# Attention and triangle layers on one core: the first scores of the second head pair moved to a later place in the first period

## The chip, the cores and the metric

The kernel runs on one core of a Trainium2 chip. The metric is the device time of one execution in microseconds; three executions of the kernel before took 3711.04, 3712.01 and 3713.63 us, so the median is 3712.01 us. The engines are named as the profile names them: PE is TensorE (PEld its weight loads), DVE is VectorE, ACT is ScalarE, POOL is GpSimd, SP is SyncE, which here issues most of the transfers.

## The reference

Two layers run one after the other on x of shape (4, 64, 64, 256), in float32. Layer 0 is self-attention over the 4096 tokens of each of the four images. Layer 1 treats each 64 x 64 image as a grid of pairs and lets edges (i, l) and (l, j) meet:

```python
# layer 0
f = xt @ Wf + bf ; g = xt @ Wg + bg ; v = xt @ Wh + bh
beta = softmax(einsum('bqd,bkd->bqk', g, f), axis=-1)
x = x + (einsum('bqk,bkd->bqd', beta, v) @ Wo + bo).reshape(b, h, w, c)
# layer 1: 8 heads of 32
q, k, v1, v2 = (x @ W).reshape(B, N, N, H, d_k) for W in (Wq, Wk, Wv1, Wv2)
scores = einsum('bilhd,bljhd->biljh', q, k) / sqrt(d_k)
att = softmax(scores, axis=2)
out = einsum('biljh,bilhd,bljhd->bijhd', att, v1, v2)
h = layer_norm(x + out.reshape(B, N, N, E) @ Wo)
h = layer_norm(relu(h @ W1 + b1) @ W2 + b2 + h)
```

## The kernel before

**Stages.** The four images go through one after the other. For each, `layer0` computes the attention (8 blocks of 512 tokens) and writes y, q, k, v1 and v2 of layer 1 to DRAM. Then a *triangle stage* computes layer 1's scores, weights and triple product for that image. In the first triangle stage (`first_layer1`) the projections of the later images' layer 0 are computed alongside. In the other three (`next_layer1`) the layer norms and the perceptron of the previous image run alongside. The last image's norms and perceptron follow on their own at the end (`alone`).

**The triangle stage.** The 8 heads form 4 pairs, the 64 rows i form 8 groups: 32 steps. Each step makes eight products (`product`, word R, L955): DVE or POOL multiplies a 128 x 64 slice of weights by a 128 x 2048 block of v2 into a tile. DVE's tiles are R (three buffers), POOL's are Rp (two). `accumulate` (word A, L965) contracts each product over l on PE into one of two PSUM tiles "acc" per step, one for products 0 to 3, the other for 4 to 7. `take` (word T, L975) copies an acc out by ACT. POOL makes products 5 to 7 of step 0 in every stage.

**Weights.** `sums` (word S) adds up a step's exponentials on DVE, `weights` (W) scales them on ACT into "es", `turn_weights` (t) transposes them on PE, `copy_weights` (c) copies POOL's share out as attP, and `stationary` (V) fills the stationary operand from v1 and fetches a later step's v1.

**Scores.** `scores` (word sp, L853) computes a quarter of a pair's scores with 64 small matmuls into a PSUM tile "sp". `take_scores` (words e, L863) writes its two halves through Exp to the tile S on ACT. The pair's q and k are fetched by `fetch_qk` (L820, L823). Pair 0's scores are made at the end of `layer0`. The fetch of pair 1's q and k is issued there too, near the end, after the last scores of pair 0 have been issued, since both pairs use the same two buffers. Word sp of period 1 is the first quarter of pair 1.

**The order.** Nothing reorders the work: each engine runs what the program gives it in that order. The order is written out by hand as lists of words, `ORDER` for stages two to four (a period is two steps) and `ORDER0` for the first (four steps). A word's number after the slash is how many periods late it runs: in period p, "A05/1" accumulates product 5 of step 0 of period p - 1. Period 0 of a stage has almost nothing to do, as most words are one or two late. Period 1 is the first with products. In it the words that act are, in order, for stages two to four:

```
R05 S1 sp e0 e1 A05 R04 A04 z0 W1 R03 V1 S0 z1 t1 so R06 R00 c1 sa A03 R07 R02 A06
A02 A00 rr pp W0 R01 A07 A01 fo fa T01 R12 t0 T00 R17 h1 R13 h0 ht R16 hU A13 ...
```

Words of the alongside work here: z0, z1 are the perceptron's output matmuls (L1177), so (ACT) and sa (DVE, L1040) the norms' statistics, rr, pp the inverse roots on ACT and their polishing on POOL, fo, fa the norms' affine maps on ACT, h0, h1 the heads (L1024), ht the turning of the normed tile (L1124), hU and hT its shift and scale. In the first stage the words from the scores on are `sp0 e00 e01 P00 C00 t1 R00 P01 C01 R03 A00 R02 g0 a0 b0 R05 R07 A05 A03 ...`: P turns a fetched block of the next image, xin, on PE (L345), C copies it out (L350), g, a and b are its projections (PE L234, ACT L243, DVE L248).

**Buffers that bear on the order.** PSUM tiles of tag "a" have two slots, taken in turn by sp and acc. The three R buffers of DVE are, at the end of `layer0`, the "stage" tiles from which the last block's q, k, v1 and v2 are stored to DRAM; a product can take one only when its stores have ended.

Of the kernel before, what the change touches and what calls it, by code (L numbers as in the profile page):

```python
# [40 lines left out]


ORDER = """
    r0/1 A10/2 A11/2 m1/1 R14/2 R05/1 S1/1 R15/2 T10/2 sp/1 A14/2 A16/2 r1/1 e0/1 e1/1 A15/2 A05/1 T11/2
    R04/1 A04/1 z0/1 W1/1 R03/1 V1/1 fi/2 S0 z1/1 t1/1 so/1 R06/1 R00/1 c1/1 sa A03/1 R07/1 R02/1 A06/1
    A02/1 A00/1 rr/1 pp/1 W0 R01/1 A07/1 A01/1 fo/1 fa T01/1 R12/1 t0 T00/1 R17/1 h1/-1 R13/1 h0/-1 ht
    R16/1 hU A13/1 hT A12/1 A17/1 R11/1 c0 R10/1 m0 V0
""".split()


# [5 lines left out]
    A21/2 g1/2 S3/1 W1/1 A27/2 A23/2 A26/2 a1/2 V3/2 A24/2 P31/2 C21/2 R32/2 b1/2 m1/2 T20/2 c3/2 P30/2 C31/2  # L56
    t0/1 v2/2 n1/2 R25/2 A25/2 R33/2 sp0/1 T21/2 A32/2 C30/2 R34/2 R36/2 R30/2 A33/2 e00/1 u2/2 e01/1 o1/2 R31/2
    g2/2 P00/1 c0/1 R37/2 A34/2 A36/2 A30/2 A31/2 A37/2 V0/1 R35/2 C00/1 T30/2 t1/1 R00/1 p1/2 P01/1 a2/2 b2/2
    C01/1 A35/2 R03/1 T31/2 A00/1 R02/1 g0/1 a0/1 b0/1 R05/1 R07/1 A05/1 A03/1 v3/2 R06/1 u3/2 m0/1 S2/1 W2/1
    c1/1 v0/1 V1/1 R01/1 A02/1 n0/1 R04/1 A07/1 A01/1 A04/1 R12/1 P11/1 u0/1 P10/1 A06/1 T00/1 sp1/1 C11/1 T01/1  # L60
    R13/1 R15/1 R14/1 A13/1 e10/1 e11/1 t2/1 C10/1 R10/1 A12/1 R17/1 V2/1 A15/1 A14/1 A10/1 R16/1 R11/1 S0 R22/1
    W3/1 g3/2 c2/1 W0 A17/1 R27/1 A11/1 v1/1 R20/1 a3/2 b3/2 u1/1 o0/1 p0/1 S1 R21/1 T10/1 P20/1 t3/1 P21/1
    A16/1 T11/1 C20/1 A20/1 R23/1 A22/1 R24/1 R26/1
""".split()


# [1 line left out]
def attention_then_triangle_kernel(  # L68
# [1264 lines left out]
    def words_of(order):  # L1333
        for w in order:
            w, late = (w.split("/") + ["0"])[:2]
            yield w, int(late)

    def first_layer1(L, ahead, F):
        turned = {}
        ahead.load(0)  # L1340

        def fetched(step):
            if 24 <= step < 31:
                ahead.fetch(F, 1, step)

        own = Late(L)
        step_word, scores, take_scores = step_words(
            L, fetched, lambda step: None, lambda step: ahead.spread(F, 1, step), own
        )

        def front_word(w, s, cc):
            if not 0 <= s < ahead.n:
                return
            if w == "P":
                ahead.turned(s, cc)
                turned[s] = turned.get(s, 0) + 1
                if turned[s] == 2:
                    ahead.load(s + 1)
            elif w == "C":
                ahead.taken(s, cc)  # L1360
            elif w == "v":
                ahead.values(s)
            elif w == "u":
                ahead.valued(s)
            elif w == "g":
                ahead.factors(s)
            elif w == "a":
                ahead.factored(s)
            elif w == "b":
                ahead.parted(s)  # L1370

        for period in range(NSTEP // 4 + 3):
            for word, late in words_of(ORDER0):
                i, last = period - late, int(word[-1])
                if word[0:2] == "sp":
                    if i >= 0:
                        scores(2 * i + last)
                elif word[0] == "e":
                    if i >= 0:
                        take_scores(2 * i + int(word[1]), last)  # L1380
                elif word[0] in "RATSWVtc":
                    step_word(word[0], 4 * i + int(word[1]), last)
                elif word[0] in "mnop":
                    if 0 <= i < 4:
                        own.word(word[0], 2 * i + last)
                elif 0 <= i < 4 and int(word[1]) < 2:
                    front_word(word[0], 2 * i + int(word[1]), last)
                elif 4 <= i < 8:
                    front_word(word[0], 4 * i - 8 + int(word[1]), last)
        ahead.fetch(F, 1, NSTEP)  # L1390


    def next_layer1(b, L, rest, ahead, F):
        own = b == NB - 1
        t0 = NP * (b - 1)


        n2, n1, n0 = NP, NP + own, NP + 2 * own
        stored, held = set(), []
        mv, rs, rn, mps = {}, {}, {}, {}  # L1400

        def fetched(step):
            if F is not None and 24 <= step < 31:
                ahead.fetch(F, b + 1, step)


        def load(q, far=False):
            if q < NP or 24 + (q - NP) // 2 in stored:
                rest.load(t0 + q, far)
            else:  # L1410
                held.append((q, far))

        def was_stored(step):
            stored.add(step)
            if own and step == 26:
                held.extend((NP + q, True) for q in (2, 3, 4))
            todo, held[:] = list(held), []
            for q, far in todo:
                load(q, far)

        def moments(q):
            if q not in mv:
                mv[q] = small.tile([P, 4, 2], F32, tag="mv", name="mv")
            rest.mv = mv[q]

        def of_piece(word, q):
            tt = t0 + q
            first, second = 1 <= q < n1, 0 <= q < n2
            if word in ("h0", "h1"):
                if 2 <= q < n0:  # L1430
                    n = int(word[1])
                    rest.heads(tt, n, new=q not in mps)
                    mps.setdefault(q, {})["h", n] = True
                    if len(mps[q]) == 2 and q + 1 < n0:
                        load(q + 1)
            elif word == "sa" and first:
                moments(q - 1)
                rest.stats(rest.hps[t0 + q], 0)
            elif word == "so" and second:
                moments(q)  # L1440
                z = rest.z[t0 + q] = work.tile([P, 2, C], F32, tag="s4", name="z")
                rest.sums_of(rest.zp[t0 + q], z, rest.mv, 2)
            elif word == "rr" and second:
                moments(q)
                rest.roots(0 if q + 1 < n1 else 2, 4)
                rs[q] = rest.rs
            elif word == "pp" and second:
                moments(q)
                rest.rs = rs.pop(q)
                rest.polish(0 if q + 1 < n1 else 2, 4, nc.gpsimd, back=back_t)  # L1450
                rn[q] = rest.rn
            elif word == "fa" and first:
                rest.rn = rn[q - 1]
                rest.affine_a(tt)
            elif word == "fo" and second:
                rest.rn = rn[q]
                rest.affine_o(tt)
            elif word == "ht" and first:
                rest.turn(tt)
            elif word == "hT" and first:  # L1460
                rest.normed(tt)
            elif word == "hU" and first:
                rest.carried(tt)
            elif word in ("m0", "m1") and first:
                n = int(word[1])
                mps[q][n] = [rest.hidden(tt, fc) for fc in (2 * n, 2 * n + 1)]
            elif word in ("r0", "r1") and first:
                n = int(word[1])
                for fc, mp in zip((2 * n, 2 * n + 1), mps[q][n]):
                    rest.rectify(tt, fc, mp)  # L1470
            elif word in ("z0", "z1") and second:
                n = int(word[1])
                rest.outputs(tt, n, new=tt not in rest.zp)
                mps.setdefault(q, {})["z", n] = True
            elif word == "fi" and second:
                rest.finish(tt)

        def spread(step):
            if F is not None:
                ahead.spread(F, b + 1, step)  # L1480

        step_word, scores, take_scores = step_words(L, fetched, was_stored, spread)
        mps[1] = {}
        for period in range(NP + 4):
            for word, late in words_of(ORDER):
                i = period - late
                if word[0] in "RATSWVtc":
                    step_word(word[0], 2 * i + int(word[1]), int(word[-1]))
                elif word == "sp":
                    scores(i)  # L1490
                elif word in ("e0", "e1"):
                    take_scores(i, int(word[1]))
                else:
                    of_piece(word, i)
        assert not held
        if F is not None:
            ahead.fetch(F, b + 1, NSTEP)
# [68 lines left out]
```

## Time and profile before

| what | value |
|---|---|
| median of three executions | 3712.01 us |
| the profiled execution, its own time | 3709.58 us |
| its span, first to last instruction | 3707.8 us |
| mean granted clock of PE | 0.990 |
| DVE, POOL busy, shares of the span | 71%, 48% |
| DMA mean rate over the span | 87 GB/s |

A triangle stage is not evenly loaded. In the middle of the second one, from 1343.4 to 1640 us, PE is busy for all 296.6 us, DVE for 287.1 and POOL for 284.4, and the granted clock is 1.00. Before it, from 1280 to 1343.4, PE is busy for 54.5 of 63.4 us. The chain of waits is followed back from the last instruction, and each of its pieces says what the next one waited for. In a timeline, a line is a run of like instructions with its start, its length, its engine and line, and in brackets how long the engine was idle ahead of it and what ended that.

### The profile page before, as it was taken

What the parts mean: (1) busy time and instruction counts of PE and PEld (TensorE: products, weight loads), DVE (VectorE), ACT (ScalarE), POOL (GpSimd) and SP (SyncE); (2) the same over time, 40 slices, a digit from 0 to 9 for tenths busy, and PEclk for the clock granted to TensorE, in tenths of its full rate; (3) what the DMA queues carried; (4) which work ended last, traced back from release to release, by engine and by line L of the source; (5) the groups of instructions that cost most, each with busy time, mean ns of one, the idle gap of its engine ahead of it and who ended that gap; (6) DMA issues with size and microseconds to landing.
All of it is one profiled execution on the core that took longest, in us unless ns stands there. A gap on an engine that the chain in (4) does not pass through costs nothing.

```text
span 3707.8 us, 58485 instructions
## 1 busy us (share of the span) xinstructions
PE 3579.3 (97%) x22602; PEld 1932.9 (52%) x22602; DVE 2641.4 (71%) x2078; ACT 1917.9 (52%) x4257; POOL 1761.7 (48%) x918
## 2 busy tenths in 40 slices
PE   9999899989999999998999999999899999999998
PEld 6555444444555555554455555554355555555477
DVE  4555499996555479999555449999755455999976
ACT  3333456554333367675433347676533435677654
POOL 5000199895000069999100019999700005999920
PEclk9999999999999999999999999999999999999999
DMA  9111566566111344425311153333511125432221
GB/s 149 47 46 46 138 163 165 147 160 158 51 51 49 102 107 94 97 51 97 74 49 51 48 142 89 75 90 65 117 42 50 51 70 138 97 89 51 68 65 56
DMA packets 461232, 324.01 MB, mean 87 GB/s; under 512 B 299984, under 2 KB 418512, under 8 KB 451600
## 3 DMA queue, kind: packets, MB, share of 16 engines
q1 hardware_dynamic: 411904, 293.21, 29.8%
q0 software_dynamic: 36160, 19.94, 4.7%
q10 hardware_dynamic: 12880, 7.01, 0.7%
q8 instruction: 181, 2.97, 0.3%
q14 instruction: 107, 0.88, 0.1%
HBM read 176.37 MB, written 143.65 MB: 86 GB/s over the span
## 4 chain that ended last, share of the span: by engine, by line
PE 80%; POOL 9%; DMA 4%; issue 3%; DVE 3%; ACT 1%; SPq 0%; ACTq 0%; POOLq 0%; DVEq 0%
PE o L552 24%; PE acc L965 17%; PE proj L609 8%; POOL Rp L955 7%; PE s L531 6%; PE mp L1157 5%; PE zp L1177 5%; PE sp L853 3%; PE hp L1024 2%; PE v1p L641 2%; PE y L594 2%; DVE R L955 1%; PE att L907 1%; DMA k<-k 1%; PE den L569 1%
## 5 line engine op out<-in xcount | busy, mean ns | idle before, releaser
L955 POOL TENSOR_TENSOR Rp<-attP,v 128x2048 f32<-128x2048 f32 x328 | 1491.3, 4574 | 432.0 <-ACT attP L915 354.0
L955 DVE TENSOR_TENSOR R<-att,v 128x2048 f32<-128x2048 f32 x696 | 1548.8, 2274 | 111.0 <-PE acc L965 67.6
L552 PE MATMUL o<-e,v 128*128 128x512 f32 x2048 | 920.5, 592 | 0.0
L559 DVE TENSOR_TENSOR esum<-esum,e 128x2048 f32<-128x2048 f32 x224 | 512.9, 2290 | 485.8 <-ACT e L541 482.8
L965 PE MATMUL acc<-R,wsel 128*32 128x512 f32 x5568 | 701.6, 601 | 16.1 <-DVE R L955 7.9
L541 ACT ACTIVATE e<-s 128x1024 f32<-128x1024 f32 x512 | 496.9, 1026 | 323.5 <-PE s L531 163.4
L552 PEld LDWEIGHTS o<-e,v 128*128 128x128 f32 x2048 | 388.5, 190 | 391.5 <-issue 369.8
L1085 POOL TENSOR_SCALAR nt<-mv 128x4 f32<-128x4 f32 (+1 forms) x51 | 9.8, 193 | 1216.5 <-DVE mv L1041 1204.1
L531 PE MATMUL s<-gT,fT 128*128 128x512 f32 x1024 | 374.1, 486 | 8.2 <-ACT e L541 4.9
L965 PE MATMUL acc<-Rp,wsel 128*32 128x512 f32 x2624 | 348.1, 603 | 20.7 <-POOL Rp L955 20.1
L975 ACT COPY ao<-acc 128x1024 f32<-128x1024 f32 x256 | 254.6, 1021 | 177.9 <-PE acc L965 167.1
L965 PEld LDWEIGHTS acc<-R,wsel 128*32 128x32 f32 x5568 | 155.2, 110 | 357.3 <-issue 280.9
L531 PEld LDWEIGHTS s<-gT,fT 128*128 128x128 f32 x1024 | 191.9, 190 | 143.7 <-issue 107.5
L890 ACT ACTIVATE es<-S,rd 128x64 f32<-128x64 f32 x1024 | 257.8, 336 | 15.9 <-DVE rd L882 14.4
L571 DVE RECIPROCAL rec<-den 128x512 f32<-128x512 f32 x32 | 107.4, 3357 | 214.4 <-PE den L569 214.4
L1157 PE MATMUL mp<-hT,w 128*128 128x256 f32 x1024 | 249.5, 389 | 0.7 <-ACT hT L1129 0.7
L1177 PE MATMUL zp<-w,hid 128*128 128x256 f32 x1024 | 245.3, 385 | 0.8 <-ACT hid L1166 0.8
L1157 PEld LDWEIGHTS mp<-hT,w 128*128 128x128 f32 x1024 | 186.9, 190 | 101.1 <-ACT attP L915 36.0
L1177 PEld LDWEIGHTS zp<-w,hid 128*128 128x128 f32 x1024 | 186.1, 191 | 63.9 <-issue 30.2
L621 ACT COPY st<-proj 128x512 f32<-128x512 f32 x98 | 57.5, 587 | 304.9 <-PE proj L609 169.8
L965 PEld LDWEIGHTS acc<-Rp,wsel 128*32 128x32 f32 x2624 | 81.0, 110 | 201.5 <-issue 128.6
L863 ACT ACTIVATE S<-sp 128x512 f32<-128x512 f32 x128 | 130.0, 1119 | 98.2 <-PE sp L853 98.2
(176 smaller groups left out, 3597.9 us busy)
## 6 DMA issues: line engine op xcount, KB each, us to landing
v<-v2d SPq DMA_DIRECT2D x44, 512.0 KB
v1c<-v1d SPq DMA_DIRECT2D x128, 128.0 KB
aT<-ao SPq DMA_DIRECT2D x1024, 16.0 KB
A<-aT SPq DMA_DIRECT2D x256, 64.0 KB
out_dram<-z SPq DMA_DIRECT2D x63, 256.0 KB
y<-yT SPq DMA_DIRECT2D x56, 256.0 KB
q<-st SPq DMA_DIRECT2D x56, 256.0 KB
k<-k SPq DMA_DIRECT2D x28, 512.0 KB
```

The lines of the kernel that those rows point to most:

```text
L531: nc.tensor.matmul(s_ps[r // 2][:, r % 2, :], fT[tt][:, ts(r * 4 + n, P)], gT[qb // 4][:, ts(qb % 4, QB)], start=True, stop=not safe,)
L541: nc.scalar.activation(e[g][:, 2 * j : 2 * j + 2, :], s_ps[j], AF.Exp)
L552: nc.tensor.matmul(o_ps[qb], F.v[tt][:, r * 4 + n, :], es[:, r, :], start=(k == 0 and r == 0), stop=(k == 7 and r == 3),)
L559: nc.vector.tensor_tensor(esum[qb], esum[qb], es, ALU.add)
L609: nc.tensor.matmul(ps, w[:, cc, rows], y(qb, cc), start=(cc == 0), stop=(cc == 1))
L863: nc.scalar.activation(self.S[pair][:, :, l0 : l0 + 8].rearrange("p i l -> p l i"), sp[:, lh], AF.Copy if self.safe else AF.Exp,)
L890: nc.scalar.mul(e[:, i, :], rows[:, i, :], rec[:, i : i + 1])
L955: eng.tensor_tensor(R, src.unsqueeze(1).to_broadcast([P, D, N]), v2[h], ALU.mult)
L965: nc.tensor.matmul(acc[32 * c : 32 * c + 32, n % 2, :], w[:, n, c, 16 * h : 16 * h + 32], R[:, ts(c, 8), :].rearrange("p d j -> p (d j)"), ...
L975: nc.scalar.copy(self.ao[step][:, ts(np, 2)].rearrange("p k d j -> p k (d j)"), self.acc[step][np])
L1157: nc.tensor.matmul(self.mp[:, fc % 2, :], w1_sb[:, cc, ts(fc, P)], self.hT[tt][:, cc, :], start=(cc == 0), stop=(cc == 1),)
L1177: nc.tensor.matmul(zp[:, n, :], self.hid[tt][:, fc, ts(n, P)], w2_sb[:, fc, :], start=(fc == 0), stop=(fc == 3 and tt not in self.hT2),)
```

## The change

The word sp of the first period is split off. The first quarter of pair 1's scores now has words of its own, sf with f0 and f1 for its two evictions (sf0, f0, f1 in the first stage). They act only where the quarter is the first, and sp, e0 and e1 act on all quarters but that. In `ORDER`, sf stands after T00, f0 after R13, f1 after ht. In `ORDER0`, sf0 stands ahead of A00, f0 after g0, f1 after R05. All other words keep their order.

```diff
 ORDER:
-    r0/1 ... S1/1 R15/2 T10/2 sp/1 A14/2 A16/2 r1/1 e0/1 e1/1 A15/2 A05/1 ...
-    ... fa T01/1 R12/1 t0 T00/1 R17/1 h1/-1 R13/1 h0/-1 ht R16/1 hU A13/1 ...
+    r0/1 ... S1/1 R15/2 T10/2 sp/1 A14/2 A16/2 r1/1 e0/1 e1/1 A15/2 A05/1 ...
+    ... fa T01/1 R12/1 t0 T00/1 sf/1 R17/1 h1/-1 R13/1 f0/1 h0/-1 ht f1/1 R16/1 hU A13/1 ...
 ORDER0:
-    ... C01/1 A35/2 R03/1 T31/2 A00/1 R02/1 g0/1 a0/1 b0/1 R05/1 R07/1 A05/1 ...
+    ... C01/1 A35/2 R03/1 T31/2 sf0/1 A00/1 R02/1 g0/1 f0/1 a0/1 b0/1 R05/1 f1/1 R07/1 A05/1 ...
 first_layer1:
                 if word[0:2] == "sp":
-                    if i >= 0:
+                    if 2 * i + last > 0:
                         scores(2 * i + last)
                 elif word[0] == "e":
-                    if i >= 0:
+                    if 2 * i + int(word[1]) > 0:
                         take_scores(2 * i + int(word[1]), last)
+                elif word[0:2] == "sf":
+                    if i == 0:
+                        scores(0)
+                elif word[0] == "f":
+                    if i == 0:
+                        take_scores(0, last)
 next_layer1:
-                elif word == "sp":
-                    scores(i)
-                elif word in ("e0", "e1"):
-                    take_scores(i, int(word[1]))
+                elif word in ("sp", "sf"):
+                    if (i == 0) == (word == "sf"):
+                        scores(i)
+                elif word in ("e0", "e1", "f0", "f1"):
+                    if (i == 0) == (word[0] == "f"):
+                        take_scores(i, int(word[1]))
```

More of the change, by code (lines that the diff above doesn't have):

```diff
@@ L43 @@
 ORDER = """
[L44 to L47, printed above, removed]
+    r0/1 A10/2 A11/2 m1/1 R14/2 R05/1 S1/1 R15/2 T10/2 sp/1 A14/2 A16/2 r1/1 e0/1 e1/1 A15/2 A05/1 T11/2 R04/1
+    A04/1 z0/1 W1/1 R03/1 V1/1 fi/2 S0 z1/1 t1/1 so/1 R06/1 R00/1 c1/1 sa A03/1 R07/1 R02/1 A06/1 A02/1 A00/1
+    rr/1 pp/1 W0 R01/1 A07/1 A01/1 fo/1 fa T01/1 R12/1 t0 T00/1 sf/1 R17/1 h1/-1 R13/1 f0/1 h0/-1 ht f1/1 R16/1
+    hU A13/1 hT A12/1 A17/1 R11/1 c0 R10/1 m0 V0
 """.split()
@@ L58 @@
     g2/2 P00/1 c0/1 R37/2 A34/2 A36/2 A30/2 A31/2 A37/2 V0/1 R35/2 C00/1 T30/2 t1/1 R00/1 p1/2 P01/1 a2/2 b2/2
[L59 to L63, printed above, removed]
+    C01/1 A35/2 R03/1 T31/2 sf0/1 A00/1 R02/1 g0/1 f0/1 a0/1 b0/1 R05/1 f1/1 R07/1 A05/1 A03/1 v3/2 R06/1 u3/2
+    m0/1 S2/1 W2/1 c1/1 v0/1 V1/1 R01/1 A02/1 n0/1 R04/1 A07/1 A01/1 A04/1 R12/1 P11/1 u0/1 P10/1 A06/1 T00/1
+    sp1/1 C11/1 T01/1 R13/1 R15/1 R14/1 A13/1 e10/1 e11/1 t2/1 C10/1 R10/1 A12/1 R17/1 V2/1 A15/1 A14/1 A10/1
+    R16/1 R11/1 S0 R22/1 W3/1 g3/2 c2/1 W0 A17/1 R27/1 A11/1 v1/1 R20/1 a3/2 b3/2 u1/1 o0/1 p0/1 S1 R21/1 T10/1
+    P20/1 t3/1 P21/1 A16/1 T11/1 C20/1 A20/1 R23/1 A22/1 R24/1 R26/1
 """.split()
```

## The prediction

> **What bounds the kernel now.** I read the page's busy shares first, then the chain that ended last, then TensorE's waits, and then the timelines of TensorE and VectorE around the first period of each triangle stage.
>
> ```profile
> PE 3579.3 (97%) x22602; PEld 1932.9 (52%) x22602; DVE 2641.4 (71%) x2078; ACT 1917.9 (52%) x4257; POOL 1761.7 (48%) x918
> ...
> PE 80%; POOL 9%; DMA 4%; issue 3%; DVE 3%; ACT 1%; SPq 0%; ACTq 0%; POOLq 0%; DVEq 0%
> ```
>
> TensorE (PE) is busy for 97% of the span and carries 80% of the chain. An idle microsecond of PE is therefore a microsecond of the kernel, unless something else is late just after it. PE's longest wait in total:
>
> ```profile
> PE sp L853 <- DMA k<-k: 29.2, 8, 4.6
> ```
>
> These are eight waits of the scores matmuls for q and k of the second head pair, two in each of the four triangle stages: 5.5 us in the first stage, 7.7, 8.0 and 7.9 in the others. The scores are the "sp" that the change moves. PE's timeline, second stage:
>
> ```profile
> 1317.49 0.38 PE L1029 MATMUL hp<-ident,yc 128*128 128x128 f32 x2
> 1321.10 0.38 PE L853 MATMUL sp<-q,k 32*64 32x64 f32 x2 [3.22 <-DMA k<-k]
> 1325.99 2.02 PE L853 MATMUL sp<-q,k 32*64 32x64 f32 x62 [4.51 <-DMA k<-k]
> 1327.94 1.63 PE L965 MATMUL acc<-Rp,wsel 128*32 128x512 f32 x8
> ...
> 1336.62 1.90 PE L965 MATMUL acc<-R,wsel 128*32 128x512 f32 x16
> ...
> 1343.36 1.07 PE L965 MATMUL acc<-R,wsel 128*32 128x512 f32 x8
> ```
>
> The reader should see PE stop at 1317.87 and go on at 1325.99. The question is what PE could do in that time. VectorE (DVE), same stretch:
>
> ```profile
> 1314.56 4.49 DVE L955 TENSOR_TENSOR R<-att,v 128x2048 f32<-128x2048 f32 x2 [3.92 <-DMA yc<-y]
> ...
> 1326.95 2.29 DVE L955 TENSOR_TENSOR R<-att,v 128x2048 f32<-128x2048 f32 x1 [7.07 <-DMA v2d<-stage]
> ...
> 1330.15 0.18 DVE L1041 BATCH_NORM_AGGREGATE mv<-st 128x2 f32<-128x6 f32 x1
> 1330.51 2.29 DVE L955 TENSOR_TENSOR R<-att,v 128x2048 f32<-128x2048 f32 x1 [0.18 <-PE acc L965]
> ```
>
> DVE stands still for 7.07 us in the same gap, for another transfer. Its third product (R00) needs the third R buffer. That one still holds "stage", whose last store (v2d<-stage, issued by ScalarE at 1316.36) ends at 1326.9. In the third and fourth stage this wait is 7.16 and 7.01 us and ends at 2215.33 and 3105.42, each 0.7 us after the scores got their data. The first stage has another wall, in the chain of waits:
>
> ```profile
> 440.02 12.60 DMA xin<-in_x_dram
> 452.62 0.14 issue
> 452.76 1.09 PE tp L345 x4
> ```
>
> The word after the scores there (P00, the turning of xin) waits for xin, which lands at 452.62. The scores end at 452.6, so they fill a wait that is there anyway.
>
> [...] nothing of PE's later work fills the gap. [...] from 1318 to 1322.2 the engines are busy by 1.01 of their time at 215 GB/s, with the q and k loads, the A loads and the v2d store under way. Moving a matmul does not make that store land earlier. [...]
>
> ```profile
> 1322.30:1329.00 6.70, 3.01 (x70) 2.25 (x74) 2.05 (x1) 0.94 (x2) 1.31 (x1) 0.50 0.64 132
> 1329.10:1331.00 1.90, 1.90 (x15) 0.71 (x8) 1.65 (x6) 1.89 (x6) 1.24 (x1) 0.99 0.75 206
> ```
>
> These are two stretches of the busy table: a stretch, its length, the busy time of PE, PE's weight loads, DVE, ScalarE and GpSimd, then the granted clock, the DMA share and GB/s. The clock is 0.50 until 1329. After the stall it stays at half for 4.8 us in the first stage, and for 3.1, 5.4 and 6.1 us in the others. At half clock the scores' 64 small matmuls cost what they always do (1.9 to 2.0 us), but a group of eight accumulations takes 1.7 us, not 0.87.
>
> **The change part by part.** No instruction is added or removed. 64 matmuls (1.91 us) and two Exp evictions (1.99 us) move, once per stage. The scores issue no DMA (only every fourth quarter does), so SyncE's and GpSimd's queues keep their order. The S that they feed is first read by sums of step 8, in the second period of stage one and the fourth of the others, behind three later quarters, so being late costs nothing by itself.
>
> *Stages two to four* (numbers of the second). Without the scores PE is free at 1317.87. The first accumulation, A05, needs the first of GpSimd's two products, begun at 1314.61 and 9.00 us long together: 1319.1. Then A05 and A04 (0.87 + 0.97), both output words z (3.99), t1 (0.53), A03 and A06 (0.89 + 0.85) bring PE to 1327.3. ScalarE is idle there for 11.72 us and does W1 earlier, so t1 finds its weights. Next is A02, which needs R02. DVE has to do R00 first, not before 1326.95 (2.2), the norm statistics (to 1330.3), and R02 (2.25): 1332.6. So PE waits anew, some 5.4 us, now for DVE. From 1332.7: A02, A00, A07, A01 took 3.55, t0 0.5, the moved scores 1.91, the heads 2.16, ht 0.53. A13 starts at 1341.35 instead of 1343.36: a gain of 2.0, not 7.7. Third stage: the statistics end at 2218.7, R02 at 2220.95, A13 at 2229.7 instead of 2233.11, gain 3.4. There R02 had waited 1.54 us for a PE at half clock, which goes. Fourth: 3119.8 instead of 3123.53, gain 3.7. Together 9.1 us.
>
> The clock takes part of it back. The new idle stretch of 5.4 us is as good for a fall as the old one, and what follows it now is accumulation, not scores. With the clock at half for 3.1 to 6.1 us, half of that time is lost: 1.5 to 3.1 us a stage, I take 2.4, 7.2 in all. Bounds: 0, if the clock doesn't fall, and 10. Net for these stages: -1.9 us.
>
> The scores' PSUM slot ("a", two slots) is now the one that A05 to A07 filled, so they wait for T01 on ScalarE, behind rr, the GpSimd polish and fo, fa. By the same durations T01 ends at about 1336.2, 0.5 us before it is needed: nothing, with up to 2 us a stage if that cover is gone.
>
> *First stage.* P00 stays at 452.76, and P01 ends at 455.43 as before. Then come the scores (1.92), so A00 starts at 457.35, not 455.43: 1.9 us lost, as they no longer fill the wait. More follows: A05 takes the PSUM slot that the scores hold until f1. On ScalarE f1 stands behind a0, which needs g0's matmuls, behind A00. A00 ends at 458.2 (459.05 at half clock), g0 0.9 later, a0 0.65, f1 1.0: A05 at 460.8 to 461.6 instead of 457.19. The chain runs through A05 (457.37, acc x16), so this goes to the end: +3.6 to +4.4, I take 4.0. Floor 1.9, ceiling 5.
>
> **Sum:** 4.0 - 9.1 + 7.2 = +2.1 us. The profiled execution took 3709.58 us (span 3707.8, 1.8 outside it), 2.4 below the median of 3712.01. On the median the forecast is 3714.1.
>
> **Rivals.** (a) The waits for k go and nothing takes their place: 29.2 us, and some 4 us of half clock, 3712 - 33 = 3679. For it speaks PE's 97%. Against it stand DVE's 7.07 us in the same gap and xin. Chance 0.05. (b) The v2d store lands some 3 us or more earlier, or DVE's lag is met by less PE idling, and the clock doesn't fall: stages two to four give 4 to 7 us each, 3695 to 3704, take 3700. [...] Against: no transfer ahead of that store is moved. Chance 0.08. (c) Slower: the moved scores sit in stages two to four behind T01, PE waiting for ScalarE's chain before them. It decides when T01 ends later than 1336.7. With 2 us a stage on top of the forecast: 3714.1 + 6 = 3720. For it: only 0.5 us of cover, and fo waits for the polish. Against: the same order of words had no such wait before, and half clock delays the matmuls as much. Chance 0.17. (d) My forecast, gain and loss nearly cancel: 0.70.
>
> **How the numbers follow.** This kernel can tell 0.2% (7.4 us) from no change. (a) and (b) are faster: 0.13. (d) stays within: 0.70. (c) is slower: 0.17. With stage one at 1.9 and no fall of the clock (d) ends at 3704.8; with both at their ceilings at 3718. The range that leaves a tenth on each side: 3705.5 to 3720.
>
> **What would show it.** Right: PE's waits for k at about 5 us of 29 (the first scores of a stage, if at all); a new wait of A02 for DVE, about 5 us in each of the stages two to four, with clock 0.50 after it; R00 still ending its wait for v2d<-stage near 9 us after the last heads; in the first stage tp waiting 8 us for xin, and A05 1.5 us for ScalarE's S. Wrong: DVE's R00 starting at once, no fall of the clock, or A05 in the first stage at its old distance from P00.

## The result, and the profile after

| | before | changed |
|---|---|---|
| median of 20 executions each, same chips | 3713.59 us | 3715.12 us |
| lowest, highest | 3710.88, 3717.55 us | 3710.02, 3718.76 us |
| span of the profiled execution | 3707.8 us | 3714.7 us |

The ratio of the times is 1.0004, with a 95% interval of 0.9998 to 1.001: between 0.7 us faster and 3.7 us slower, so no change that this measurement can tell. The two profiled executions lie 6.9 us apart, more than the medians do. The changed one (3716.47) was 1.4 us above its median, the other (3709.58) 4.0 us below.

The page of the changed kernel, its busy shares and its chain:

```profile
PE 3583.0 (96%) x22602; PEld 1932.3 (52%) x22602; DVE 2640.8 (71%) x2078; ACT 1918.6 (52%) x4257; POOL 1761.1 (47%) x918
...
PE 80%; POOL 8%; DMA 4%; DVE 3%; issue 3%; ACT 1%; SPq 1%; ACTq 0%; POOLq 0%; DVEq 0%
```

PE's waits (total in us, times, longest), first one line of the kernel before, then those of the changed one:

```profile
PE acc L965 <- DVE R L955: 7.9, 15, 1.4
```

```profile
PE acc L965 <- POOL Rp L955: 24.6, 22, 2.7
PE acc L965 <- DVE R L955: 23.0, 19, 5.3
PE tp L345 <- DMA xin<-in_x_dram: 10.0, 2, 8.0
```

Of the 29.2 us that PE waited for k nothing is left. In their place stand 15.1 us more for DVE's R (23.0 against 7.9), with one wait of about 5 us in each of the stages two to four, and one wait of 8.0 us for xin in the first stage. PE's timeline in the second stage's first period:

```profile
1328.13 0.38 PE L1029 MATMUL hp<-ident,yc 128*128 128x128 f32 x2
1329.84 1.07 PE L965 MATMUL acc<-Rp,wsel 128*32 128x512 f32 x8 [1.33 <-POOL Rp L955]
...
1337.10 1.04 PE L965 MATMUL acc<-Rp,wsel 128*32 128x512 f32 x8
1343.45 3.50 PE L965 MATMUL acc<-R,wsel 128*32 128x512 f32 x16 [5.30 <-DVE R L955]
```

After the last heads (hp, up to 1328.51) PE now waits 1.33 us for POOL's product and then does 8.3 us of work without a pause. Then it stands for 5.30 us, at A02. The 16 accumulations that follow (A02, A00) take 3.50 us; in the kernel before they took 1.90. DVE in the same stretch:

```profile
1325.19 4.49 DVE L955 TENSOR_TENSOR R<-att,v 128x2048 f32<-128x2048 f32 x2 [3.92 <-DMA yc<-y]
...
1337.84 2.29 DVE L955 TENSOR_TENSOR R<-att,v 128x2048 f32<-128x2048 f32 x1 [7.32 <-ACT z L1059]
...
1341.13 11.06 DVE L955 TENSOR_TENSOR R<-att,v 128x2048 f32<-128x2048 f32 x5
```

R00 starts 7.3 us late, as before, 12.65 us after the first two products began (12.39 in the kernel before). The name of the releaser has changed: ScalarE's z here and in the third stage, v2d<-stage in the fourth stage of this same profile. Such a name is the event that came last by the profile, so it need not be the cause; the runs e4 and e5 below decide which of the two it is. The first stage, PE, with A05 in the kernel before ahead of the changed kernel's lines:

```profile
457.19 1.04 PE L965 MATMUL acc<-Rp,wsel 128*32 128x512 f32 x8
```

```profile
453.49 1.09 PE L345 MATMUL tp<-ident,xin 128*128 128x128 f32 x4 [8.01 <-DMA xin<-in_x_dram]
...
456.21 2.03 PE L853 MATMUL sp<-q,k 32*64 32x64 f32 x64
458.18 1.55 PE L965 MATMUL acc<-R,wsel 128*32 128x512 f32 x8
459.55 0.61 PE L234 MATMUL gf<-xT,wg 128*32 128x128 f32 x16
459.99 0.61 PE L234 MATMUL gf<-xT,wf 128*32 128x128 f32 x16
462.32 1.06 PE L965 MATMUL acc<-Rp,wsel 128*32 128x512 f32 x8 [1.72 <-issue]
```

P00 waits 8 us for xin. From P00 to A05 it is now 8.83 us (462.32 less 453.49); it was 4.43 (457.19 less 452.76). Some 0.5 us of that is the clock: A00 ran at half in this profile (1.55 us, granted clock 0.50 up to 459.1), and at full in e2, e7 and e11 (1.06 to 1.07), where P00 to A05 took 8.35. The timeline puts A05's wait down to nothing it knows ("issue"); ScalarE's shows what stands there:

```profile
458.33 1.04 ACT L863 ACTIVATE S<-sp 128x512 f32<-128x512 f32 x1 [1.42 <-PE sp L853]
460.67 0.37 ACT L243 ACTIVATE gf<-gf,bias_g 128x128 fp32r<-128x128 f32 x1 [1.31 <-PE gf L234]
460.94 0.36 ACT L243 ACTIVATE gf<-gf,bias_f 128x128 fp32r<-128x128 f32 x1
461.19 1.03 ACT L863 ACTIVATE S<-sp 128x512 f32<-128x512 f32 x1
```

Between f0 at 458.33 and f1 at 461.19 ScalarE waits 1.31 us for PE's gf. f1 ends at 462.2, and A05 starts at 462.32: it takes the PSUM slot that f1 has just emptied.

**Where the time went, stage by stage.** If the start of each matmul in one trace is set against that of the same matmul in the other, the distance between the two runs can be followed through the kernel (us, changed less before):

```
just behind the first layer 0       +0.9
after the first stage's period 1    +5.2
at the start of the second stage   +10.6
behind the second stage's period 1 +10.5
behind the third's                  +8.4
behind the fourth's                 +7.3
```

The first stage costs 4.3 us in its first period and 5.4 later, the second stage gives 0.1, the third 2.2, the fourth 1.1 with the end of the third and the layer 0 ahead of it. So in these two profiles the small sum is made of two parts of opposite sign.

Of the loss later in the first stage, the larger part falls at one place, some 425 to 435 us behind layer 0's end: 3.6 us of a wait, and the half clock behind it (0.50 from 847.7 to 851.4; in the kernel before the same matmuls ran at 1.00). The kernel before, then the changed one:

```profile
838.78 2.05 PE L357 MATMUL vp<-wh,xT 128*128 128x128 f32 x16 [1.92 <-ACT va L364]
```

```profile
847.67 3.78 PE L357 MATMUL vp<-wh,xT 128*128 128x128 f32 x16 [5.49 <-ACT va L364]
```

```profile
846.52 0.37 ACT L243 ACTIVATE gf<-gf,bias_g 128x128 fp32r<-128x128 f32 x1 [9.12 <-DMA ahgf<-gf]
```

PE waits for a copy by ScalarE (va), and ScalarE stood 9.12 us for a store of g and f, where it stood 5.12 us in the kernel before. The move is not what sets this wait. In the five other runs with the first stage's scores in their old place and xin late (e1, e4, e5, e6, e8) PE stands there for 3.50 to 5.83 us, and with the scores moved (e2, e7, e11) for 4.73 to 4.94. The 1.92 us of the first profile are the exception.

### The profile page after: what moved, and what is told of

It reads as the page before. It is cut to its first block, busy times and chain, and to the rows that moved or that the text cites. A ratio compares the mean times of both kernels' runs of the same rounds, so it can differ in the third digit from the quotient of the medians.

```text
span 3714.7 us, 58482 instructions
## 1 busy us (share of the span) xinstructions
PE 3583.0 (96%) x22602; PEld 1932.3 (52%) x22602; DVE 2640.8 (71%) x2078; ACT 1918.6 (52%) x4257; POOL 1761.1 (47%) x918
## 4 chain that ended last, share of the span: by engine, by line
PE 80%; POOL 8%; DMA 4%; DVE 3%; issue 3%; ACT 1%; SPq 1%; ACTq 0%; POOLq 0%; DVEq 0%
PE o L552 23%; PE acc L965 17%; PE proj L609 8%; POOL Rp L955 7%; PE s L531 6%; PE mp L1157 5%; PE zp L1177 5%; PE sp L853 3%; PE hp L1024 3%; PE v1p L641 2%; DVE R L955 2%; PE y L594 2%; PE att L907 1%; PE den L569 1%; PE htp L1124 1%
## 5 line engine op out<-in xcount | busy, mean ns | idle before, releaser
L552 PE MATMUL o<-e,v 128*128 128x512 f32 x2048 | 919.9, 592 | 0.0
L552 PEld LDWEIGHTS o<-e,v 128*128 128x128 f32 x2048 | 387.8, 189 | 391.6 <-issue 369.9
L1166 ACT ACTIVATE hid<-mp,b_sb 128x256 f32<-128x256 f32 x256 | 105.3, 470 | 117.7 <-PE mp L1157 117.7
```

The costliest lines, as they stand in the source:

```text
L552: nc.tensor.matmul(o_ps[qb], F.v[tt][:, r * 4 + n, :], es[:, r, :], start=(k == 0 and r == 0), stop=(k == 7 and r == 3),)
```

## The experiments

"e1" to "e11" are the beginnings of the runs' labels. Two measures come up again and again, both worked out from the traces: the *stage time*, from the last value matmul of one image's layer 0 (L552) to that of the next image, and *A13's distance*, from that same matmul to the first accumulation of step 1, which in stages two to four is the first thing on PE behind everything that the change touches. A13's distance before: 65.8, 67.3 and 67.5 us in stages two to four; changed: 65.7, 65.1 and 66.9. A *stay* is an unbroken time at half clock.

e3, e5, e7, e9 and e11 were executed once each (3709.25, 3713.51, 3706.65, 3708.49 and 3715.79 us). Executions of one kernel lie 9 us apart and more (3710.02 to 3718.76 us for the changed one), so these runs are read by the waits and distances of their traces and not by their times. Where a run's kernel has more lines, its line numbers are shifted: L861 in e6 and e8 and L855 in e9 are the scores of L853.

**e1 and e2: each half of the change alone.** e1 takes ORDER and `next_layer1` from the changed kernel, e2 takes ORDER0 and `first_layer1`.

```diff
 e1, on the kernel before:
-    ORDER  ... sp/1 ... e0/1 e1/1 ... T00/1 R17/1 h1/-1 R13/1 h0/-1 ht R16/1 ...
+    ORDER  ... sp/1 ... e0/1 e1/1 ... T00/1 sf/1 R17/1 h1/-1 R13/1 f0/1 h0/-1 ht f1/1 R16/1 ...
 e2, on the kernel before:
-    ORDER0 ... T31/2 A00/1 R02/1 g0/1 a0/1 b0/1 R05/1 R07/1 A05/1 ...
+    ORDER0 ... T31/2 sf0/1 A00/1 R02/1 g0/1 f0/1 a0/1 b0/1 R05/1 f1/1 R07/1 A05/1 ...
```

> Only stages two to four have their first scores moved; the first stage is as before. Theory (loss in stage one, small gain in the others): about 2 to 4 us faster than before, 3710 on a median of 3713.6; by place, no difference until the end of the first stage beyond what single executions differ by, then -0.1, -2.2 and -0.6 us in the three later stages, within 1.5 us each [...]. PE waits for DVE's R about 5 us in each. Rival (the later stages gain nothing, all is noise): the same as before within 1 us. Rival (waits for k simply go): 20 us faster or more.

> Only the first stage has its first scores moved. Theory: A05 comes 8.8 us after P00 instead of 4.4, so 3 to 5 us slower than before, 3717 to 3718; the further 5.8 us that the changed kernel's profile lost later in the first stage is not of the change, and need not come back here. Rival (that further loss belongs to the change): 9 to 10 us slower. Rival (the first stage's loss is absorbed later in the stage): the same as before.

e1 took 3708.87 us against 3713.7, a ratio of 0.9988 (0.9979 to 0.9996): 4.8 us faster, between 1.5 and 7.8. e2 took 3717.07, 1.0009 (1.0 to 1.0018): 3.4 us slower, between 0 and 6.7. The two halves have opposite signs, as the stage sums said. Their sum is 1.4 us faster, and the whole change measured 1.5 us slower; the intervals are too wide to make anything of that. A13 came 0.0, 2.0 and 2.5 us earlier in e1 than in the kernel before. The last is outside what was expected (0.6, within 1.5): in the fourth stage the stay behind the new wait was 3.4 us in e1 and 6.8 in the changed kernel. PE's waits in e1 hold the whole new wait of stages two to four and, for k, only the first stage's:

```profile
PE acc L965 <- DVE R L955: 22.9, 19, 5.3
...
PE sp L853 <- DMA k<-k: 5.4, 2, 4.6
```

**e3: the first stage's evictions ahead of g0.**

```diff
 e3, on the changed kernel:
-    ORDER0 ... A00/1 R02/1 g0/1 f0/1 a0/1 b0/1 R05/1 f1/1 R07/1 A05/1 ...
+    ORDER0 ... A00/1 R02/1 f0/1 f1/1 g0/1 a0/1 b0/1 R05/1 R07/1 A05/1 ...
```

> The changed kernel, but in the first stage f0 and f1 stand ahead of g0, so that ScalarE evicts the scores before it comes to a0. Theory (A05 waits for f1 behind a0): PE's wait of 1.7 us before A05 goes, and A05 comes 6.9 to 7.2 us after P00, not 8.8. Rival (A05 waits for its product or for something else): still 8.8 us.

A05 came 6.95 us after P00 (458.11 less 451.16), within the expected 6.9 to 7.2. PE's lines in e3:

```profile
451.16 1.09 PE L345 MATMUL tp<-ident,xin 128*128 128x128 f32 x4 [7.88 <-DMA xin<-in_x_dram]
...
458.11 1.06 PE L965 MATMUL acc<-Rp,wsel 128*32 128x512 f32 x8 [0.31 <-issue]
```

The wait fell from 1.72 to 0.31 us. A00 ran at full clock here (1.06 us), so the fair comparison is with the 8.35 us of e2, e7 and e11: evicting first saves 1.4 us. So the price in the first stage has two main terms: 2.0 us of scores that no longer fill the wait for xin, and 1.7 us of waiting for a PSUM slot whose last eviction stood behind an instruction that needed PE. Of the second, e3 takes away 1.4.

**e7: other matmuls in the new gap.** z0's and z1's output matmuls (and their turns) are made a second time between A06 and A02 and write the same values again.

```diff
 e7, on the changed kernel, in next_layer1:
                     step_word(word[0], 2 * i + int(word[1]), int(word[-1]))
+                    if word == "A06" and period == 1:
+                        for n in range(2):
+                            rest.outputs(t0, n, new=False)
```

> The changed kernel with the output matmuls of z0 and z1 made a second time in the gap between A06 and A02, in stages two to four (16 matmuls and 8 turns a stage, 3.9 us, written over with the same values). Theory (A02 waits for DVE's R02, and the gap costs the clock): A02 starts at the same distance after the last heads (15.0 us in stage two), the clock stays at 1.00, and A02 to A01 take 3.6 us instead of 5.2, 5.1 and 6.6: A13 1.6, 1.6 and 3.0 us earlier, some 6 us in all. Rival (the clock doesn't matter there, DVE sets A01): A13 at the same distance. Rival (PE has no real gap): A13 3.9 us later.

With some 4 us more work on PE per stage, A13 came *earlier*: its distance is 64.2, 63.9 and 63.9 us, 1.5, 1.2 and 3.0 us less than in the changed kernel. A02 itself did not move: in the second stage it starts 14.99 us behind the last heads, and in the changed kernel 14.94, both times with R02.

```profile
1339.08 1.92 PE L965 MATMUL acc<-R,wsel 128*32 128x512 f32 x16 [1.25 <-DVE R L955]
```

The busy table has the reason. Its columns are the stretch, its length, the busy time of PE, PE's weight loads, DVE, ScalarE and GpSimd, then the granted clock, the DMA share and GB/s. First the changed kernel:

```profile
1338.20:1343.20 5.00, 0.00 (x0) 0.00 (x0) 4.93 (x6) 1.85 (x9) 1.73 (x7) 1.00 0.53 133
1343.40:1346.60 3.20, 3.15 (x16) 0.79 (x20) 3.20 (x2) 2.16 (x6) 3.20 (x2) 0.50 0.00 0
1346.70:1349.00 2.30, 2.30 (x24) 0.77 (x16) 2.30 (x2) 1.12 (x2) 2.30 (x2) 1.00 0.00 0
```

and the same place in e7:

```profile
1333.70:1339.00 5.30, 4.13 (x24) 3.38 (x20) 5.23 (x7) 2.02 (x9) 1.91 (x8) 1.00 0.51 124
1339.10:1342.60 3.50, 3.50 (x32) 0.91 (x32) 3.50 (x2) 2.77 (x7) 3.50 (x2) 1.00 0.03 7
```

The changed kernel does 16 matmuls in 3.20 us at half clock, e7 does 32 in 3.50 at full clock. The gap is real and the clock is its second price: 5.7 us over the three stages. From the second stage to the end e7 took 2421.1 us, 5.4 less than the changed kernel.

**e4 and e5: the store away from the R buffer.** The last k and v2 of layer 0 are stored from tiles of tag "st" instead of the third "stage" tile. e4 does it on e1, e5 on the kernel before. `late` is true for the first image alone, which keeps its k store as it was.

```diff
-        proj(last, "k", 1, None, stage[2][:, 0, :], nc.scalar)
+        proj(last, "k", 1, None, stage[2][:, 0, :] if late else None, nc.scalar)
-            proj(last, "v2", 1, None, stage[2][:, 1, :], nc.scalar)
+            proj(last, "v2", 1, None, None, nc.scalar)
```

> As e1 (only stages two to four moved), and there the last k and v2 of layer 0 are stored from tiles of their own, not from the R buffer that DVE's third product R00 needs. Theory (R00 waits for that store, and PE behind it): R00 starts about 5 us after the first two products' end minus the sums, at once, PE's 5 us wait for DVE before A02 goes, and A13 comes 5.4 us earlier than before in stage two (the scores then wait up to 1.9 us for T01) or 7.3 us (if they don't), and 1.5 us more than that in stages three and four: 19 to 25 us faster than before, 3689 to 3695. Rival (R00 waits for ScalarE's z, as the changed kernel's trace names it in two stages): R00 still starts some 7 us late, and the time is that of e1. Rival (the data of q and k hold PE anyway): PE waits for k at the new place.

> The kernel before with the same stores apart, the scores in their old place. Theory (two waits stand beside each other, for k and for the store, and the first alone holds PE here): DVE's R00 starts some 7 us earlier, PE's waits for k stay at 7.7 to 8.0 us a stage, and A13 comes within 1 us of before. Rival (the store alone is what costs, the scores' place does not matter): 10 us faster or more.

e4 took 3695.53 us against 3710.56, 0.9957 (0.994 to 0.9973): 15.0 us faster, where 19 to 25 were expected. A13 came 3.8, 5.3 and 5.7 us earlier than before; the expectation had 5.4, 6.9 and 6.9 with the wait for T01 in it. What is missing is for the most part the clock, some 1.8 us in the second stage (shown with e8). e5 took 3713.51 in a single execution: no gain that shows. DVE in e4, second stage:

```profile
1317.59 4.49 DVE L955 TENSOR_TENSOR R<-att,v 128x2048 f32<-128x2048 f32 x2 [3.92 <-DMA yc<-y]
...
1322.82 2.25 DVE L955 TENSOR_TENSOR R<-att,v 128x2048 f32<-128x2048 f32 x1
```

R00 follows the sums at once, at 1322.82, before PE has even begun z's matmuls (1324.09). So z can't be what held it, and the stores from that buffer were. (The two, of k and of v2, were moved together; which of them counts was not tried.) In e5 R00 starts at once, too, but PE still waits for k, 28.5 us in all, and DVE then stands for PE 8.82 us:

```profile
PE sp L853 <- DMA k<-k: 28.5, 8, 4.7
```

```profile
1336.31 2.29 DVE L955 TENSOR_TENSOR R<-att,v 128x2048 f32<-128x2048 f32 x1 [8.82 <-PE acc L965]
```

So there are two walls beside each other, two transfers that two engines wait for in the same gap. Getting round the one alone (e1) gives 5 us, removing the other alone (e5) nothing, both together 15 us. A13's distance in e5, 67.5, 66.3 and 67.1 us, is that of before within 1.7 us, where 1 was expected; the differences go with the clock's stays there (10.2, 6.8 and 10.2 us, against 6.8, 10.2 and 10.2 before). What is late next in e4 is the PSUM slot, as one of the rivals had it, and behind the scores the clock is at half (0.50 from 1338.60 to 1341.80):

```profile
1336.15 2.08 PE L853 MATMUL sp<-q,k 32*64 32x64 f32 x64 [1.59 <-ACT ao L975]
1338.16 1.81 PE L1024 MATMUL hp<-wo,A 128*128 128x256 f32 x4
```

**e6: other work ahead of the scores instead.** The scores keep their place ahead of A05; five words that need neither k nor the scores' slot go ahead of them, in the first period of stages two to four alone.

```diff
 e6, on the kernel before, first period of next_layer1:
-    ... T10/2 sp/1 ... e0/1 e1/1 A15/2 A05/1 ... A04/1 z0/1 W1/1 R03/1 V1/1 fi/2 S0 z1/1 t1/1 so/1 ...
+    ... T10/2 W1/1 V1/1 z0/1 z1/1 t1/1 sp/1 ... e0/1 e1/1 A15/2 A05/1 ... A04/1 R03/1 fi/2 S0 so/1 ...
```

> The kernel before, but in the first period of stages two to four W1, V1, z0, z1 and t1 stand ahead of the scores, which keep their place ahead of A05 and their PSUM slot. PE then does 4.5 us of other work while k is under way, and the scores fill the rest of DVE's wait. Theory: PE waits for k some 3.5 us a stage instead of 7.9, A02 starts when R02 is ready (1332.7 in stage two's time before), and A13 comes 3.9 us earlier than before in stage two, 5.4 in three and four at full clock: 9 to 15 us faster, 3699 to 3705. Rival (the clock falls all the same and A05 to A06 run at half): 3 to 6 us faster.

```profile
1331.73 1.98 PE L861 MATMUL sp<-q,k 32*64 32x64 f32 x62 [3.48 <-DMA k<-k]
...
1339.18 1.92 PE L973 MATMUL acc<-R,wsel 128*32 128x512 f32 x16 [0.71 <-DVE R L963]
```

e6 took 3700.92 us against 3710.56, 0.9973 (0.9963 to 0.9983), about 10 us faster. A13's distance is 63.0, 63.3 and 63.0 us: 2.8, 4.0 and 4.5 us less than before, short of the 3.9, 5.4 and 5.4 that were expected at full clock. PE waits for k 3.48 us in the second stage, and the clock still fell, for 3.4 to 6.8 us a stage, but part of that lay under DVE's wait (0.71 us is left of it at A02). By these distances e6 beats moving the scores alone (e1: 65.9, 65.3 and 65.0): here they fill the wait, and the other work no longer stands behind them.

**e8: T01 right behind A07.** On e4, in the first period of stages two to four.

```diff
-    ... W0 R01/1 A07/1 A01/1 fo/1 fa T01/1 R12/1 t0 T00/1 sf/1 ...
+    ... W0 R01/1 A07/1 T01/1 A01/1 fo/1 fa R12/1 t0 T00/1 sf/1 ...
```

> As e4, and in the first period of stages two to four T01 stands right behind A07, ahead of A01, fo and fa, so that the scores' PSUM slot comes free before they are reached. Theory (in e4 the scores wait for T01 on ScalarE, 1.59 us in stage two): that wait goes, A13 comes 1.6 us earlier than in e4 in each of the three stages, and up to 1.7 us more where the clock no longer falls there: 5 to 9 us faster than e4, 3686 to 3691. Rival (heads and ht then wait for fa, which is now later on ScalarE): the same as e4.

```profile
1332.90 1.98 PE L861 MATMUL sp<-q,k 32*64 32x64 f32 x64
1334.81 1.13 PE L1032 MATMUL hp<-wo,A 128*128 128x256 f32 x4
```

e8 took 3689.95 us against 3713.53, 0.9936 (0.9919 to 0.9952). A13's distance is 58.65 us in all three stages, 3.4, 3.4 and 3.1 us less than in e4, twice the 1.6 us of the wait. The other half is the clock: in e4 it fell in each of these periods (0.50 from 1338.60 to 1341.80 in the second stage), in e8 in none; the mean granted clock of their profiled executions was 0.992 and 0.994. From the scores' start to A13, the same matmuls took 6.49 us in e4's second stage (1336.15 to 1342.64) and 4.71 in e8's (1332.90 to 1337.61).

**e9, e10: xin early in the first stage.** The first xin is loaded at the start of layer 0's last block; e9 is the changed kernel with this alone, e10 has the whole change with all four of the above: stores apart (e4), T01 early (e8), xin early (e9), and f0 and f1 ahead of g0 (e3).

```diff
 layer0, first image:
+            if qb == last and k == 0 and late:
+                rest.early()
 first_layer1:
-        ahead.load(0)
```

> The changed kernel with the load of the first xin issued at the start of layer 0's last block, not behind the loads of q and k. Theory (in the first stage the scores' old place lay inside the wait for xin, which is why moving them cost time): P00 no longer waits 8 us, the moved scores then wait for k instead, and A05 comes about 12 us after the weights' last turn, where it came 12.6 us after before and 16.8 in the changed kernel; so the move no longer costs time there. Rival (xin is not what holds PE, ScalarE's and DVE's work is): A05 still 16 us after.

> The whole change (both stages' lists) with all four mends: stores apart, T01 early, xin early, f0 and f1 ahead of g0. Theory: the gain of e8 in stages two to four, and 2 to 3 us in the first stage against before: 3683 to 3689. Rival (the first stage's later part takes the gain back): as e8.

In e9 A05 starts 12.8 us after the end of the weights' last turn ahead of P00 (457.52 less 444.74), where it was 12.6 before and 16.85 in the changed kernel. P00 no longer waits:

```profile
444.57 0.60 PE L345 MATMUL tp<-ident,xin 128*128 128x128 f32 x4
446.67 1.91 PE L909 MATMUL att<-ident,es 128*128 128x128 f32 x4 [1.50 <-ACT es L892]
...
450.21 2.02 PE L855 MATMUL sp<-q,k 32*64 32x64 f32 x62 [0.39 <-DMA k<-k]
```

xin was the wall, and with it away the moved scores cost nothing against the kernel before (the first stage took 866.4 us). The kernel before with xin early alone was not run, so how much of this xin gives without the move stays open. e10 took 3686.45 us against 3713.53, 0.9926 (0.991 to 0.9943). That is the lowest time here, 27 us below the kernel before; from e8 it can't be told apart. Of the 2 to 3 us that the first stage was to give against the kernel before, its first period gives 2.9 in e10's profile (91.4 us to step 4's start, against a mean of 94.3), but the whole stage, 867.1 us, is no shorter than the mean of 867.5, as that run's rival had it.

**e11: the changed kernel once more.**

> The changed kernel once more, for a second profile of the first stage. Theory (the 5.8 us that its first profile lost after the first period of stage one is the spread of single executions): stage one from layer 0's end to the next layer 0's end takes between 868 and 876 us, with 3 to 5 us of it lost in the first period. Rival (it belongs to the change): 875 us again.

The first stage took 873.2 us. Taking the profiles of all runs together, the first stage's time is:

```
first stage (us)       whole stage             to step 4's start     the rest
moved:  changed, e2, e7, e11
        875.2 875.0 871.6 873.2   mean 873.7   98.2 (96.8 to 99.2)   775.5 (773.5 to 778.3)
as before:  before, e1, e4, e5, e6, e8
        865.6 867.4 866.8 869.4 869.2 866.7
                                  mean 867.5   94.3 (92.8 to 95.4)   773.2 (770.2 to 776.4)
```

In the first period the two groups lie apart, by 3.9 us in the means. Of the 5.4 us that the first profile lost later, 2.3 are left in the means, and there the groups overlap. e2 was to tell whether that later loss belongs to the change: its stage was as long as the changed kernel's (875.0 us), but e7 and e11, with the same first stage, were shorter. The wait behind va, shown above, lies in one range for both places (3.50 to 5.83 us with the old, 4.73 to 5.49 with the new), with the kernel before alone outside it. Whether the move has a small cost later in the first stage stays open. Stages two to four, with what follows them, took 2426.5 us on average in the five profiles where their scores are moved and nothing else is (changed, e1, e3, e9, e11) and 2429.1 in the two where they are not (before, e2): 2.6 us less, with the groups just apart (2425.4 to 2427.9, and 2428.0 to 2430.3).

## Why the prediction was right

Forecast were 3714.1 us on a median of 3712.0, so 2.1 us slower. The 20 executions gave 1.5 us slower. The mechanism was right; that the sums agree to 0.6 us is in part luck, since single terms are off by more. By its steps:

- *PE's idle time for k is not free time; DVE stands behind a store in the same gap.* Right. The new wait was put at 5.4 us; it is 5.30, 4.77 and 5.03. e4 shows the stores from that buffer as its cause, and the trace before had named one of them in all three stages. One sign was off: some 5 us of waiting for k were to be left, and none was, as the first stage's scores, too, stand behind a longer wait (for xin) at their new place.
- *A13 at full clock 2.0, 3.4 and 3.7 us earlier.* e7, with the clock kept up, has A13 at 64.2, 63.9 and 63.9 us, against 65.8, 67.3 and 67.5 before: 1.6, 3.4 and 3.6.
- *The clock takes 2.4 us of that back in each stage, 7.2 in all.* Measured as the distance between e7 and the changed kernel: 1.5, 1.2 and 3.0, together 5.7. The bounds of 0 and 10 hold it. That the clock would fall in the new gap, too, was the author's estimate: in the trace before it was 0.50 from 1322.3 to 1329, in the old gap and behind it. The changed kernel's trace shows the fall: behind the gaps of 5.30, 4.77 and 5.03 us the clock is 0.50 for 3.41, 3.41 and 6.83 us. The sizes came from the stays of the kernel before. Net, these stages were to give 1.9 us; they give 2.6 in the means above.
- *The PSUM slot costs nothing in stages two to four.* Right: the moved scores start behind t0 without a wait, in e7 at full clock, too. The slot became the limit only when DVE's wait was gone (e4).
- *First stage: 4.0 us, from 1.9 for the scores that no longer fill xin's wait and the rest for f1 behind a0.* A05 came 4.4 us later in the profile with A00 at half clock, and 3.9 later in the three with A00 at full clock, as the forecast's two cases had it; the first period takes 3.9 us longer in the means. e9 shows the first term, e3 the second. What the forecast did not have are the 2.3 us that the means show later in the stage, if they belong to the move.
- *The rivals.* That the waits for k simply go (3679) is what PE's 97% alone would say; with both walls and the wait for T01 away, e8 and e10 come 24 and 27 us below the kernel before, where this rival had 33. That the moved scores wait for T01 was wrong for this kernel and right for e4.

Gain and loss thus nearly cancel, each within about 2 us of its term. The measured parts, 3.9 us in the first period less the 2.6 of the later stages, give 1.3 us; with the 2.3 us later in the first stage they give 3.6. The timed 1.5 us, between -0.7 and 3.7, decides nothing between the two.

## What to carry to other kernels

When an engine that is busy for 97% of the span waits, first look at what the engines that feed it do in the same gap, and which buffers and transfers they wait for. Moving the waiting work helped here by no more than the distance to the second wall, and work that fills a wait costs nothing where it stands. Moved work also takes its slot in a buffer ring and its evictions' place in another queue with it; ask of both what now stands ahead of them.

## What the runs showed of the hardware

- In the traces of the kernel before and the changed one the granted clock of PE took only the values 1.00 and 0.50. Its stays at half, but for the one that the end of each run cuts off, lasted 3.41 us (8 in the kernel before, 9 in the changed one), 6.83 (1 and 2), 10.24 (3 and none) or 13.65 (none and 1), multiples of 3.41. It fell not only after stretches in which PE was idle throughout, as in the changed kernel from 1338.20 to 1343.20. In e4 it fell after one in which PE was busy for 2.25 of 3.30 us, almost all of it with the scores' small matmuls (32 rows by 64 columns, 64 elements). Whether it is their size that counts was not tried:

```profile
1335.10:1338.40 3.30, 2.25 (x65) 2.08 (x66) 3.30 (x2) 2.03 (x4) 3.30 (x2) 1.00 0.04 8
1338.60:1341.80 3.20, 3.20 (x10) 2.43 (x9) 0.03 (x1) 1.63 (x2) 3.20 (x1) 0.50 0.11 21
```

- Those small matmuls hardly feel the clock: 64 of them took 2.03 us at half clock in the changed kernel's first stage and 1.98 at full clock (the kernel before, at 1407.30). The four turns of a 128 x 128 tile do: 1.09 us there, 0.60 at full clock (the kernel before, at 500.47). So it matters which work stands behind a gap: in the old order it was the scores that ran into the half clock (2.02 us for 62 of them at 0.50, in the second stage of the kernel before), in the new one accumulations (3.50 us for 16 at half clock, 1.90 at full).
- Repeating work could save time: some 4 us of matmuls, made for a second time in a gap, brought the next step forward by 1.2 to 3.0 us (e7).
- In the gap for k PE began nothing of its later work: with the scores ahead of it, A05 began 10.07 us behind the second stage's last heads (1327.94 less 1317.87, the kernel before), and with the scores moved 1.33 us behind them (1329.84 less 1328.51, the changed kernel).
